# A two-layer graph attention kernel: the last product's blocks written by ScalarE before x is added by accumulating transfers, the first norm taken tile by tile, and another fixed order

## The chip, the cores and the metric

The kernel runs on one core of a Trainium2 chip. The metric is the device time of one execution in microseconds. The kernel before takes 2771.11 us (median of 3 executions, 2768.26 to 2773.03).

## What is computed

There are 32 graphs of 512 nodes with 512 features. Each is normalised, passed through ReLU and two graph attention layers (4 heads of 256, then 1 head of 512), and added to its input. All of it is float32.

```python
def gat_layer(x, mask, W, a_src, a_dst, bias, concat):
    xl = (x @ W).reshape(B, N, H, F)
    asrc = jnp.einsum('bnhf,hf->bnh', xl, a_src)
    adst = jnp.einsum('bnhf,hf->bnh', xl, a_dst)
    e = jax.nn.leaky_relu(asrc[:, :, None, :] + adst[:, None, :, :], 0.2)
    e = jnp.where(mask[..., None], e, NEG_INF)
    attn = jax.nn.softmax(e, axis=1)
    out = jnp.einsum('bsdh,bshf->bdhf', attn, xl)
    ...
h = jnp.maximum(_layernorm(x, axis=-1), 0.0)
mask = (adj > 0) | jnp.eye(N, dtype=bool)[None]
h = jax.nn.elu(gat_layer(h, mask, W1, att_src1, att_dst1, b1, concat=True))
h = gat_layer(h, mask, W2, att_src2, att_dst2, b2, concat=False)
return x + h
```

## The kernel before

**The work of a graph.** Four products are made on TensorE, each as seven smaller ones (a Winograd form of Strassen's scheme): the first projection (`project1`), the first layer's sums over neighbours (`gather1`, four heads), the second projection (`project2`) and the second layer's sums (`gather2`). The sums and differences of blocks that this scheme needs before a product are made by VectorE; its results come out of the 8 PSUM banks (`mm`) by ScalarE or VectorE, and some of them go back into another bank by ScalarE, to be added to.

**The softmax.** `first` finds the softmax's sums row by row: ScalarE forms `l` from a broadcast row `as`, VectorE masks it, ScalarE exponentiates it. The result goes through DRAM to become a row that every partition has (`drr<-rr`, `rr<-drr`). `second` builds the attention block `p` on VectorE from `rr`, adds the mask to it by accumulating transfers from DRAM (`p<-dm`, queue of POOL), and exponentiates it on ScalarE. `p` is what `gather1` and `gather2` multiply with.

**The last product and the residual.** `gather2` makes four output tiles of 128 rows, each from two column halves. `residual` first loads the four tiles of x into the four slots `t` (SP's queue). Each partial product that comes out of a bank is then multiplied by the softmax's share and added into its half of a tile by one VectorE instruction (in `put`, cost `PUT`). After the last of them the tile is stored by SP and its slot is given back. The slots `t` also hold VectorE's differences t1 and t2 for `gather1`, so the next graph's `gather1` waits for the stores.

**The turn.** After the first graphs, a turn of the loop does `gather1` and `second` of one graph, `project1` of the next but one, `gather2` of the current one, the norm of the third next (`norm`, `norm_turn`), and `project2`. The parts of a turn are interleaved.

**What sets the order.** Every function only records jobs with their engine, their cost and the keys they read and write (`Program.add`). `Program.order` then lays the jobs out. In the kernel before it is a planner: it runs through a time of its own, with costs, DMA delays (`KIND`) and the numbers `PLACES` as ranks, and lets each engine take the ready job of the lowest rank. The numbers of one turn serve for all turns. Each engine runs its jobs in the order that comes out, and a job that waits holds up everything behind it on its engine or queue.

**The start.** The norm of graph 0 computes the statistics of its four tiles, one power on POOL for all four (`L770`), then ScalarE's ReLU, TensorE's transposes (`identf`) and the copies into `ht`. The first products need `ht`, four blocks of W1 and the columns that VectorE computes from W1 and the attention vectors (`scores1`, 8 instructions for a first pair of columns).

Of the kernel before, what the change touches and what calls it, by code (L numbers as in the profile page):

```python
# [10 lines left out]
F32 = mybir.dt.float32  # L11
# [4 lines left out]
OP = mybir.AluOpType  # L16
# [28 lines left out]
class Banks(Slots):  # L45
# [171 lines left out]
)  # L217
LATE = {
   
}  # L220

# [1488 lines left out]
```

## Time and profile before

| | us |
|---|---|
| median of 3 executions | 2771.11 |
| lowest, highest | 2768.26, 2773.03 |
| profiled execution, whole time | 2769.33 |
| its span, first to last instruction | 2767.6 |
| VectorE busy | 2558.2 (92%) |
| ScalarE busy | 2229.1 (81%) |
| POOL busy | 313.1 (11%) |
| DMA, share of 16 engines: queue of SP / queue of POOL | 42.4% / 25.1% |

The durations come from the profiled execution, which is 1.8 us under the median of the runs. Each 128x128 by 128x256 float32 matmul shows as two instructions, which overlap in the pipeline: a single one lasts about 380 ns, while a new one starts about every 210 ns. So TensorE's busy time says when it had something in work, not how fast it went; how many matmuls a stretch of fixed length holds says that. Names such as `t<-mm,rs,t` say what an instruction writes and reads. "p<-dm" is the transfer that adds the mask, "as<-das" and "rr<-drr" are the broadcasts.

### The profile page before, as it was taken

Reading aid. Unit: us, or ns where it says so; the run is one execution under the profiler, and the core shown is the slowest. Engines: PE = TensorE matmul, PEld = TensorE weight load, DVE = VectorE, ACT = ScalarE, POOL = GpSimd, SP = SyncE. Lnnn points to the kernel's source line nnn. Section 1 sums busy time; section 2 is a strip of 40 time slices with the busy share of each in tenths; the row PEclk is TensorE's granted clock in tenths of the full one; section 3 lists DMA queues with packets and bytes.
Section 4 is the critical chain, followed back from the end, with each engine's and each line's share of the span. In section 5 each row is a group of like instructions: output and inputs, shape, how many; then the busy total and the mean of one; then the engine's idle time right before and its main releaser. Section 6 shows DMA issues by size and latency. Waiting matters only on the chain. (4 is left out here: it accounts for less than half of the span.)

```text
span 2767.6 us, 42320 instructions
## 1 busy us (share of the span) xinstructions
PE 2742.4 (99%) x12924; PEld 2371.8 (86%) x12924; DVE 2558.2 (92%) x6732; ACT 2229.1 (81%) x4907; POOL 313.1 (11%) x356
## 2 busy tenths in 40 slices
PE   7999999999999999999999999999999999999999
PEld 6788888888888888888888888888888888888887
DVE  8999999999999999999999999999999999999996
ACT  5978888778887788877888877888778788788883
POOL 0110111101111111111011111111111111101110
PEclk9999999999999999999999999999999999999999
DMA  8657766667666667667676766766676767767563
GB/s 232 176 157 182 203 167 184 187 176 194 182 183 179 182 176 196 178 175 195 173 201 172 182 187 178 192 186 180 180 188 175 201 167 180 195 165 208 162 171 112
DMA packets 375864, 502.14 MB, mean 181 GB/s; under 512 B 222804, under 2 KB 227668, under 8 KB 375636
## 3 DMA queue, kind: packets, MB, share of 16 engines
q1 hardware_dynamic: 329844, 332.68, 42.4%
q0 software_dynamic: 45792, 166.74, 25.1%
q8 instruction: 103, 1.69, 0.3%
q14 instruction: 125, 1.02, 0.1%
HBM read 316.41 MB, written 51.31 MB: 133 GB/s over the span
## 5 line engine op out<-in xcount | busy, mean ns | idle before, releaser
L531 PE MATMUL mm<-w_sb,hs 128*128 128x257 f32 (+3 forms) x2908 | 667.0, 367 | 5.1 <-ACT mm L514 3.3
L531 PEld LDWEIGHTS mm<-w_sb,hs 128*128 128x128 f32 x2908 | 539.7, 190 | 87.7 <-ACT mm L514 6.7
L525 POOL DMA_DIRECT2D p<-dm x314 | 273.2, 875 | 2295.0 <-DVE p L517 764.3
L531 PE MATMUL mm<-w_sb,ht 128*128 128x258 f32 x2112 | 528.6, 382 | 2.7 <-ACT mm L514 2.5
L531 PE MATMUL mm<-p,xl 128*128 128x258 f32 (+1 forms) x1984 | 495.8, 383 | 0.1
L531 PE MATMUL mm<-w_sb,h 128*128 128x257 f32 x2056 | 477.8, 379 | 0.0
L517 DVE SCALAR_TENSOR_TENSOR p<-rr,z 128x512 f32<-128x512 f32 (+1 forms) x636 | 456.0, 742 | 2.4 <-DMA rr<-drr 2.4
L531 PEld LDWEIGHTS mm<-w_sb,ht 128*128 128x128 f32 x2112 | 393.7, 190 | 63.6 <-ACT mm L514 6.4
L514 ACT ACTIVATE p<-p,z 128x512 f32<-128x512 f32 (+1 forms) x636 | 433.4, 720 | 17.7 <-DVE p L517 12.4
L531 PEld LDWEIGHTS mm<-w_sb,h 128*128 128x128 f32 x2056 | 389.0, 189 | 58.4 <-ACT xl L514 0.5
L531 PEld LDWEIGHTS mm<-p,xl 128*128 128x128 f32 x1984 | 367.2, 190 | 52.7 <-issue 6.0
L514 ACT ACTIVATE mm<-mm 128x257 f32<-128x257 f32 (+2 forms) x498 | 169.8, 347 | 269.2 <-PE mm L531 236.2
L514 ACT ACTIVATE l<-as,z 128x512 f32<-128x512 f32 x516 | 354.4, 716 | 30.8 <-DMA as<-das 30.7
L514 ACT ACTIVATE l<-l,low 128x512 f32<-128x512 f32 x516 | 370.3, 721 | 7.6 <-DVE low L517 6.7
L517 DVE CUSTOM_DVE_ANT_1 l<-l,mt 128x512 f32<-128x512 f32 x516 | 346.2, 681 | 28.4 <-ACT l L514 27.4
L514 ACT ACTIVATE xl<-mm 128x258 f32<-128x258 f32 (+2 forms) x748 | 269.3, 382 | 91.4 <-PE mm L531 89.8
L514 ACT ACTIVATE h<-mm,b_sb 128x256 f32<-128x256 f32 (+1 forms) x504 | 231.0, 480 | 77.3 <-PE mm L531 76.6
L531 PE MATMUL mm<-t,hs 128*128 128x258 f32 (+1 forms) x992 | 246.1, 380 | 0.0
L517 DVE TENSOR_TENSOR xl<-xl,mm 128x258 f32<-128x258 f32 x372 | 155.3, 419 | 57.9 <-PE mm L531 48.3
L531 PEld LDWEIGHTS mm<-t,hs 128*128 128x128 f32 x992 | 185.8, 190 | 25.5 <-DVE t L517 0.2
L531 PE MATMUL mm<-xl,p 128*128 128x258 f32 (+2 forms) x752 | 189.7, 388 | 1.0 <-ACT h L514 0.6
L517 DVE SCALAR_TENSOR_TENSOR h<-xr,h 128x512 f32<-128x512 f32 x256 | 172.2, 683 | 6.1 <-ACT xr L514 6.1
(137 smaller groups left out, 3706.2 us busy)
## 6 DMA issues: line engine op xcount, KB each, us to landing
p<-dm POOLq DMA_DIRECT2D x314, 512.0 KB, 5.0
rr<-drr SPq DMA_DIRECT2D x159, 512.0 KB
x<-in_x_dram SPq DMA_DIRECT2D x129, 256.0 KB
adj<-in_adj_dram SPq DMA_DIRECT2D x128, 256.0 KB
as<-das SPq DMA_DIRECT2D x64, 512.0 KB
t<-in_x_dram SPq DMA_DIRECT2D x124, 256.0 KB
out_dram<-t SPq DMA_DIRECT2D x124, 256.0 KB
dm<-m SPq DMA_DIRECT2D x64, 256.0 KB
```

Of the source, the lines that this page charges most:

```text
L514: prog.add("ACT", cost, reads, writes, lambda: nc.scalar.activation(*a, **k))
L517: prog.add("DVE", cost, reads, writes, lambda: f(*a, **k))
L525: lambda: nc.gpsimd.dma_start(to, at, accum_op=OP.add), size,
L531: f(*a, **k)
```

## The change

**The residual.** `residual` no longer loads x, except for the last graph, whose last product is made in another way (`gather2_plain`). `put` lets ScalarE write the first partial product of each half of a tile, scaled by the share, and leaves VectorE only the second ones (products 3 and 7). When a tile is complete, a new accumulating transfer on POOL's queue adds x from DRAM to it, and the store follows.

**The first norm.** For graph 0, the epsilon, the power on POOL and the shift are done for each tile by itself; for the others they stay in one piece.

**The identity.** `identf` is no tile of its own any more but lies in a part of `hx`, which is first used otherwise when graph 1 has been transposed. The transposes therefore read the key of `hx`.

**The order.** The planner is gone. The numbers `PLACES` are new, finer by a factor of 100, and are the order itself: each engine takes its jobs in the order of their numbers.

```diff
-    identf = sbuf.tile([P, P], F32, name="identf")
-    make_identity(nc, identf)
...
+    identf = hx[SMALL[0]][:, 0, :]
+    make_identity(nc, identf)
...
-        every = [sk + (t,) for t in range(NT)]
-        rstd = st[:, :, S + A]
-        dve(TINY, every, every, nc.vector.tensor_scalar_add, rstd, st[:, :, S + 1], EPS)
-        prog.add(
-            "POOL", 1.0, every, every,
-            lambda: nc.gpsimd.tensor_tensor(rstd, rstd, half, op=OP.pow),
-        )
...
+        for ts in ([t] for t in range(NT)) if b == 0 else [range(NT)]:
+            every = [sk + (t,) for t in ts]
+            at = slice(ts[0], ts[-1] + 1)
+            rstd = st[:, at, S + A]
+            dve(TINY, every, every, nc.vector.tensor_scalar_add, rstd, st[:, at, S + 1], EPS)
+            prog.add(
+                "POOL", 1.0, every, every,
+                lambda r=rstd, n=len(every): nc.gpsimd.tensor_tensor(r, r, half[:, :n], op=OP.pow),
+            )
...
-            dma(XLOAD, [x2_key(b, 0, 0)], halves, xr, x[b, d * P : (d + 1) * P, :])
+            if b == B - 1:
+                dma(XLOAD, [x2_key(b, 0, 0)], halves, xr, x[b, d * P : (d + 1) * P, :])
+            else:
+                for c in range(2):
+                    prog.alias(xk + (c,), [xk, xk + (c,)])
...
-            dve(
-                PUT, [bk, sk, xk + (c,)], [xk + (c,)], nc.vector.scalar_tensor_tensor,
-                to, ps[:, :M], share, to, op0=OP.mult, op1=OP.add,
-            )
+            if n in (3, 7):
+                dve(
+                    PUT, [bk, sk, xk + (c,)], [xk + (c,)], nc.vector.scalar_tensor_tensor,
+                    to, ps[:, :M], share, to, op0=OP.mult, op1=OP.add,
+                )
+            else:
+                act(COPY, [bk, sk, xk], [xk + (c,)], to, ps[:, :M], AF.Copy, scale=share)
...
+                halves = [xk, xk + (0,), xk + (1,)]
+                accumulate(XADD, halves, halves, xt, x[b, d * P : (d + 1) * P, :])
                 dma(STORE, [xk, xk + (0,), xk + (1,)], (), out[b, d * P : (d + 1) * P, :], xt)
...
     def order(self):
-        jobs, rank = self.jobs, self.ranks()
...
+        jobs, rank, done = self.jobs, list(self.ranks()), []
...
+        for j in sorted(range(len(jobs)), key=lambda j: (rank[j], j)):
+            lines[jobs[j][0]].append(j)
...
+            q = min((q for q in lines if q and not left[q[0]]), key=lambda q: rank[q[0]])
+            j = q.popleft()
```

Over the whole program ScalarE gets 248 instructions more (128x256, out of PSUM), VectorE 248 fewer of them and 6 small ones more in the first norm, POOL 124 transfers of x and 3 powers more, and SP 124 loads of x fewer. TensorE's matmuls are the same in number and shape.

**POOL in a steady turn.** Before, from the mask of the second layer's `p` on, over the masks of the next graph's head 0 and head 1, the power of a norm, to the mask of head 2 (each mask in two transfers):

```order
L525 DMA p_104<-dm_121 128x1024 x2
L525 DMA p_102<-dm_120 128x1024 x2
L525 DMA p_103<-dm_120 128x1024 x2
L770 TENSOR_TENSOR stats_123<-stats_123,half 128x4
L525 DMA p_104<-dm_120 128x1024 x2
```

And now, the same stretch:

```order
L481 DMA p_101<-dm_119 128x1024 x2
L481 DMA p_102<-dm_121 128x1024 x2
L481 DMA t_108<-in_x_dram 128x512
L481 DMA t_106<-in_x_dram 128x512
L481 DMA t_107<-in_x_dram 128x512
L729 TENSOR_TENSOR stats_122<-stats_122,half 128x4
L481 DMA t_105<-in_x_dram 128x512
L481 DMA p_103<-dm_121 128x1024 x2
L481 DMA p_101<-dm_121 128x1024 x2
```

The masks of head 1, which stood ahead of the power, now stand behind it and behind all four additions of x.

**SP in a steady turn.** The four stores of the output, and the transposes (`L811`, now `L770`) that bring a later graph's normalised tiles `x` into `ht`. Before:

```order
L520 DMA rr_114<-drr_118 128x1024
L520 DMA out_dram<-t_108 128x512
L520 DMA x_90<-in_x_dram 128x512
L520 DMA out_dram<-t_106 128x512
L520 DMA out_dram<-t_109 128x512
L520 DMA out_dram<-t_107 128x512
L811 DMA_TRANSPOSE x_91<-adj_94 128x8x128
L520 DMA drr_119<-rr_115 4x8x32
L811 DMA_TRANSPOSE x_90<-adj_95 128x8x128
L520 DMA rr_115<-drr_119 128x1024
```

Now:

```order
L476 DMA x_88<-in_x_dram 128x512
L476 DMA drr_117<-rr_113 4x8x32
L476 DMA out_dram<-t_108 128x512
L476 DMA out_dram<-t_106 128x512
L476 DMA out_dram<-t_105 128x512
L770 DMA_TRANSPOSE x_87<-adj_93 128x8x128
L476 DMA out_dram<-t_107 128x512
L770 DMA_TRANSPOSE x_88<-adj_94 128x8x128
L476 DMA rr_113<-drr_117 128x1024
L770 DMA_TRANSPOSE x_89<-adj_93 128x8x128
```

The stores still stand just ahead of the transposes, but each now also waits for an addition of x on POOL's queue.

**The start, on SP's queue.** Before (`x` are graph 0's tiles, `p` the attention vectors, `w_sb` W1):

```order
L520 DMA w_sb<-in_L_gnn_W_dram 128x2x256
L520 DMA x_90<-in_x_dram 128x512
L520 DMA x_88<-in_x_dram 128x512
L520 DMA x_91<-in_x_dram 128x512
L520 DMA x_89<-in_x_dram 128x512
L520 DMA p_102<-in_L_gnn_att_src_dram 128x512
L520 DMA w_sb<-in_L_gnn_W_dram 128x2x256 x3
L520 DMA p_102<-in_L_gnn_att_dst_dram 128x512
```

Now:

```order
L476 DMA x_88<-in_x_dram 128x512
L476 DMA x_87<-in_x_dram 128x512
L476 DMA b_sb<-in_L_gnn_b_dram 128x8x1
L476 DMA x_89<-in_x_dram 128x512
L476 DMA x_90<-in_x_dram 128x512
L476 DMA w_sb<-in_L_gnn_W_dram 128x2x256
L476 DMA p_101<-in_L_gnn_att_src_dram 128x512
L476 DMA w_sb<-in_L_gnn_W_dram 128x2x256 x2
L476 DMA p_101<-in_L_gnn_att_dst_dram 128x512
L476 DMA w_sb<-in_L_gnn_W_dram 128x2x256 x5
```

The bias b1, a transfer of single 4-byte elements that was the 28th, is now third. The second attention vector is still the tenth transfer, now ahead of the fourth block of W1 instead of behind it.

More of the change, by code (lines that the diff above doesn't have):

```diff
@@ L2 @@
 from contextlib import ExitStack
-from heapq import heappop, heappush
 import concourse.bass as bass
@@ L63 @@
 PLACES = (
[153 rows of a table removed]
-)
-LATE = {
-}
[197 rows of a table added]
+)
 class Program:
-    CROSS, SAME = 0.15, 0.07
-    PAIRS = {("PE", "ACT"): 0.21, ("PE", "DVE"): 0.21, ("DVE", "POOL"): 0.58, ("POOL", "DVE"): 0.4}
-    AHEAD, MASK, OTHER = 3.5, (0.75, 1.84), 0.76
-    KIND = {
-        0.3: (0.39, 1.21, 0.1, 0.9),
-        0.76: (0.81, 1.62, 0.33, 0.64),
-        0.77: (0.44, 1.45, 0.2, 0.82),
-        0.9: (0, 1.72, 1.0, 0.41),
-        0.92: (0.48, 2.18, 0.24, 0.89),
-        0.94: (-0.2, 1.76, 0.21, 0.6),
-        1.09: (1.58, 1.56, 0.53, 0.59),
-        1.84: (0.48, 2.18, 0.24, 0.89),
-        2.23: (0.58, 1.62, 0.53, 0.4),
-    }
     ENGINES = "PE", "ACT", "DVE", "POOL", "SP"
@@ L286, in ranks @@
         turn = sum(job[1] for job in self.jobs[first : first + each] if job[0] == "PE")
-        rank, self.place = [], []
         for j in range(n):
             if j < first:
-                v, i = j, 0
+                yield PLACES[j] / 10000
             elif j < last:
-                v, i = first + (j - first) % each, (j - first) // each + 1
+                yield PLACES[first + (j - first) % each] / 10000 + turn * ((j - first) // each + 1)
             else:
-                v, i = first + each + j - last, (last - first) // each + 1
-            self.place.append(v)
-            rank.append(PLACES[v] / 100 + turn * i)
-        return rank
+                yield PLACES[first + each + j - last] / 10000 + turn * ((last - first) // each + 1)
     def order(self):
-        jobs, rank = self.jobs, self.ranks()
-        n = len(jobs)
-        after = [[] for _ in range(n)]
+        jobs, rank, done = self.jobs, list(self.ranks()), []
+        after, left = [[] for _ in jobs], [len(job[2]) for job in jobs]
         for j, job in enumerate(jobs):
@@ L305, in order @@
                 after[d].append(j)
-        left = [len(job[2]) for job in jobs]
-        ready_at, self.start, done = [0.0] * n, [0.0] * n, []
-        free, soon, ready = dict.fromkeys(self.ENGINES, 0.0), defaultdict(list), defaultdict(list)
-        wires, now, behind = {"SP": deque(), "POOL": deque()}, 0.0, {"SP": 0.0, "POOL": 0.0}
-        for j in range(n):
-            if not left[j]:
-                heappush(soon[jobs[j][0]], (0.0, j))
-        def release(j, at):
-            for s in after[j]:
-                ready_at[s] = max(ready_at[s], at(s))
-                left[s] -= 1
-                if not left[s]:
-                    heappush(soon[jobs[s][0]], (ready_at[s], s))
@@ L321, in step @@
-        def step(until):
-            nonlocal now
-            busy = [q for q in wires if wires[q] and wires[q][0][1] <= now]
-            speed = dict.fromkeys(wires, 1.0)
-            if len(busy) == 2:
-                speed["SP"], speed["POOL"] = self.kind(wires["SP"][0][0])[2:]
-            event, which = until, None
-            for q in wires:
-                if wires[q]:
-                    j, since, todo = wires[q][0]
-                    t = now + todo / speed[q] if q in busy else since
-                    if t < event:
-                        event, which = t, q
-            for q in busy:
-                wires[q][0][2] -= (event - now) * speed[q]
-                behind[q] -= (event - now) * speed[q]
-            now = event
-            if which in busy:
-                j = wires[which].popleft()[0]
-                release(j, lambda s: event + self.kind(j)[1] + LATE.get(self.place[j], 0) / 100)
-            return which is not None
@@ L344, in order @@
-        while len(done) < n:
-            t, e = float("inf"), None
-            for q in self.ENGINES:
-                if ready[q]:
-                    at = free[q]
-                elif soon[q]:
-                    at = max(free[q], soon[q][0][0])
-                else:
-                    continue
-                if q in wires:
-                    at = max(at, now + behind[q] - self.AHEAD)
-                if max(at, now) < t:
-                    t, e = max(at, now), q
-            if step(t):
-                continue
-            while soon[e] and soon[e][0][0] <= t:
-                k = heappop(soon[e])[1]
-                heappush(ready[e], (rank[k], k))
-            j = heappop(ready[e])[1]
-            self.start[j] = t
-            free[e] = t + jobs[j][1]
-            done.append(j)
-            if jobs[j][4] is not None:
-                wires[e].append([j, free[e] + self.kind(j)[0], jobs[j][4]])
-                behind[e] += jobs[j][4]
-            else:
-                release(j, lambda s: t + jobs[j][1] + self.latency(j, s))
+        lines = {e: [] for e in self.ENGINES}
@@ L371, in order @@
+        for j in sorted(range(len(jobs)), key=lambda j: (rank[j], j)):
+            lines[jobs[j][0]].append(j)
+        lines = [deque(q) for q in lines.values()]
+        while any(lines):
+            q = min((q for q in lines if q and not left[q[0]]), key=lambda q: rank[q[0]])
+            j = q.popleft()
+            done.append(j)
+            for k in after[j]:
+                left[k] -= 1
         return done
@@ L443, in tile_gat @@
     nc.scalar.preload_act_table_set("natural_log_exp_and_others")
-    identf = sbuf.tile([P, P], F32, name="identf")
-    make_identity(nc, identf)
-    diag = sbuf.tile([P, P], BF16, name="diag")
-    nc.vector.tensor_scalar(diag, identf, -1.0, BIG, op0=OP.add, op1=OP.mult)
     half = sbuf.tile([P, NT], F32, name="half")
@@ L468, in tile_gat @@
     hx = {n: sbuf.tile([P, 3, P], F32, name=f"hx{n}") for n in SMALL}
+    identf = hx[SMALL[0]][:, 0, :]
+    make_identity(nc, identf)
+    diag = sbuf.tile([P, P], BF16, name="diag")
+    nc.vector.tensor_scalar(diag, identf, -1.0, BIG, op0=OP.add, op1=OP.mult)
     rs = sbuf.tile([P, 2, 2, 2], F32, name="rs")
@@ L557, in tile_gat @@
     ROWS = {4: 1.09, 8: 2.23}
+    XADD = 1.9
     COPY, ADD, TINY = 0.266, 0.335, 0.08
@@ L790, in norm_turn @@
             pe(
-                [xk], [pk], 0.44,
+                [xk, ("hx", SMALL[0])], [pk], 0.44,
                 [(nc.tensor.transpose, (pt[:, k * P : (k + 1) * P], hn[:, k * P : (k + 1) * P], identf), {})
```

18 lines of the change are left out of this document (5 added, 13 removed), and 350 rows, old and new, of the table PLACES.

## The prediction

> **What bounds the kernel now.** I read the page first, for what TensorE leaves idle.
>
> ```profile
> span 2767.6 us, 42320 instructions
> PE 2742.4 (99%) x12924; PEld 2371.8 (86%) x12924; DVE 2558.2 (92%) x6732; ACT 2229.1 (81%) x4907; POOL 313.1 (11%) x356
> ```
>
> TensorE has work in flight in all but 25.2 us, and the change leaves its matmuls as they are. So it can win only what TensorE loses now, and the question is where that is. The table of windows gives the ends and the first turns, the table of waits who is waited for:
>
> ```profile
> core 0: us, PE busy (x) PEld busy (x) DVE busy (x) ACT busy (x) POOL busy (x), PEclk, DMA share, GB/s
> 0.00:12.06 12.06, 0.00 (x0) 0.00 (x1) 5.88 (x22) 2.15 (x3) 1.74 (x7) 1.00 0.79 235
> 12.06:60.00 47.94, 45.45 (x210) 39.02 (x211) 42.55 (x178) 27.73 (x62) 1.12 (x1) 0.96 0.88 254
> 60.00:300.00 240.00, 238.68 (x1070) 196.39 (x1069) 222.41 (x597) 203.84 (x449) 32.66 (x35) 1.00 0.66 173
> 2595.00:2695.00 100.00, 98.79 (x464) 84.77 (x463) 93.67 (x235) 84.14 (x185) 12.18 (x14) 1.00 0.63 164
> ...
> PE mm L531 <- ACT x L514: 12.1, 1, 12.1
> PE mm L531 <- ACT mm L514: 5.8, 10, 1.2
> ```
>
> 12.1 us pass before the first matmul, and most of the other waits end with a copy on ScalarE (`mm`). In the steady turns the busy time hides losses, since matmuls overlap; the number that a window of fixed length holds does not. I cut 300 to 2595 us into 27 windows of 85 us, about a turn each:
>
> ```profile
> 300.00:385.00 85.00, 85.00 (x407) 74.29 (x406) 79.68 (x208) 69.66 (x154) 9.76 (x11) 1.00 0.68 182
> ...
> 725.00:810.00 85.00, 84.56 (x402) 73.44 (x402) 79.09 (x206) 69.07 (x154) 9.76 (x11) 1.00 0.69 182
> 810.00:895.00 85.00, 84.19 (x403) 73.46 (x402) 79.73 (x207) 69.28 (x155) 9.76 (x11) 1.00 0.70 182
> ...
> 980.00:1065.00 85.00, 83.82 (x400) 72.93 (x399) 78.90 (x203) 68.36 (x153) 9.79 (x11) 1.00 0.68 182
> ...
> 2340.00:2425.00 85.00, 84.53 (x401) 73.13 (x400) 79.02 (x204) 68.95 (x154) 9.79 (x11) 1.00 0.70 183
> ...
> sum 2295.00, PE 2290.57 PEld 1998.29 DVE 2146.94 ACT 1886.80 POOL 263.62; mean PE 84.84 PEld 74.01 DVE 79.52 ACT 69.88 POOL 9.76
> ```
>
> A fed window holds 407, that is 0.209 us a matmul. The four short ones shown lack 5, 4, 7 and 6; all 27 together lack 39, or 8.1 us. That is all that the steady turns can give. What a loss looks like, on ScalarE and TensorE in the worst window:
>
> ```profile
> 1000.46 1.33 ACT L514 ACTIVATE p<-p,z 128x512 f32<-128x512 f32 x2 [1.37 <-DMA p<-dm]
> ...
> 1002.01 0.49 PE L531 MATMUL mm<-w_sb,hs 128*128 128x129 f32 x2 [1.18 <-ACT mm L514]
> ```
>
> A mask's transfer lands late, the exponential that needs it holds ScalarE, the copies behind it come late, and TensorE waits 1.18 us. ScalarE's own waits in the steady turns say which causes recur:
>
> ```profile
> ACT l L514 <- DMA as<-das: 28.3, 31, 2.3
> ACT mm L514 <- DVE t L517: 25.6, 27, 1.8
> ACT p L514 <- DMA p<-dm: 5.2, 8, 1.4
> ```
>
> Transfers again, and once a turn VectorE's write of an output block (`t`), which holds a bank that ScalarE wants to fill.
>
> **The change part by part.** First the partial products that leave VectorE. Their durations, with the nearest row for the new ScalarE form (a copy of almost the same size out of PSUM) and POOL's issue:
>
> ```profile
> L517 DVE SCALAR_TENSOR_TENSOR t<-mm,rs,t 128x256 f32<-128x256 f32 x320 | 147.3, 474 | 6.3 <-PE mm L531 5.3
> ...
> L514 ACT ACTIVATE xl<-mm 128x258 f32<-128x258 f32 x496 | 177.0, 383 | 70.5 <-PE mm L531 69.3
> ...
> L525 POOL DMA_DIRECT2D p<-dm x314 | 273.2, 875 | 2295.0 <-DVE p L517 764.3 <-DVE t L517 596.2 <-PE mm L531 450.2
> ```
>
> A turn has 12 of them; 8 move. VectorE loses 8 x 0.474 = 3.8 us a turn and goes from 79.5 to 75.7 of 85. ScalarE gains 8 x 0.383 = 3.1 us and goes from 69.9 to 72.9. Neither sets the end by its sum, so 3.8 us a turn is not the gain. What the move can give is that ScalarE no longer waits for VectorE's `t` once a turn. It can also take: a scaled copy needs the reciprocal that VectorE makes, and ScalarE, on which TensorE waits, has 12 us of air a turn instead of 15. The other half of the gain must come from the new order, which can put more work between a transfer and the instruction that waits for it. Bounds for the steady turns: 8.1 us if every loss goes, nothing if losses as many come back (worse is the third rival). I take two thirds, 5.4, since one of the three recurring waits goes for certain, and the other two are waits in a queue that an order can move.
>
> Then the additions of x. In the stretch around the end of a `gather2`:
>
> ```profile
> q0 software_dynamic: 576, 2.10, 29.9%
> ...
> p<-dm POOLq DMA_DIRECT2D x4, 512.0 KB, 5.3
> ...
> 1130.00:1160.00 30.00, 30.00 (x140) 26.14 (x139) 26.96 (x68) 27.01 (x56) 4.52 (x5) 1.00 0.73 192
> ```
>
> Four masks take 29.9% of the 16 DMA engines for 30 us, 2.24 us each. A tile of x has half a mask's bytes at its target and as many at its source, so 1.12 to 2.24 us, and four of them 4.5 to 9.0 us in a stretch that has 27% of 30 us, 8.1 us, free. The four loads that go away were issued earlier in the turn and free nothing here. The additions run after the last use of the tile, and their cover is the time until the slots `t` and the masks behind them in the queue are needed. How long that is:
>
> ```profile
> 1139.75 0.86 POOL L525 DMA_DIRECT2D p<-dm  x1 [4.17 <-PE mm L531]
> 1142.60 0.86 POOL L525 DMA_DIRECT2D p<-dm  x1 [1.99 <-DVE p L517]
> ...
> 1143.52 0.45 DVE L517 SCALAR_TENSOR_TENSOR t<-mm,rs,t 128x256 f32<-128x256 f32 x1
> ...
> 1152.42 1.34 ACT L514 ACTIVATE p<-p,z 128x512 f32<-128x512 f32 x2
> ...
> 1153.19 0.69 DVE L517 TENSOR_TENSOR t<-p 128x512 f32<-128x512 f32 x1
> ...
> 1156.07 2.76 PE L531 MATMUL mm<-t,hs 128*128 128x258 f32 x12
> ```
>
> The first mask of head 1 is issued at 1139.75 and lands some 5.3 us later, at 1145.1. Two exponentials (1.34) and VectorE's difference (0.69) must follow before TensorE uses it at 1156.07. So 1156.07 - 2.0 - 1145.1 = 9.0 us are cover. The additions take 4.5 to 9.0 of them: I cost them at nothing, with ScalarE's other work as the cover. POOL's issues, 4 x 0.875 = 3.5 us a turn on an engine that is busy for 9.8 of 85, cost nothing by themselves, and the stores behind them on SP are covered in the same way.
>
> The Trainium skill speaks against the move in one point (DMA: Bandwidth & Descriptors, section "SWDGE vs HWDGE vs iDMA"): inside a DMA engine transfers issued by GpSimd and those issued by SP stand in different queues, and the engine takes them in turn. By that, a load of x on SP's queue shared the engine with the masks, while an addition of x stands in front of them; no row here shows this sharing. Another section of that page ("Anatomy of one DMA") gives 2.0 us plus bytes over 436 GB/s for a GpSimd transfer: as an estimate 2.6 us for x and 3.2 us for a mask. The row has 5.3 us for the mask, so the measurement decides and the larger cost stands.
>
> The start. Which transfer is waited for, and what TensorE then loses:
>
> ```profile
> 13.21 0.43 DVE L517 SCALAR_TENSOR_TENSOR xr<-w_sb,p 128x256 f32<-128x256 f32 x1 [1.30 <-DMA p<-in_L_gnn_att_dst_dram]
> ...
> 14.67 1.57 PE L531 MATMUL mm<-w_sb,ht 128*128 128x258 f32 x4
> ...
> 49.40 1.65 PE L531 MATMUL mm<-w_sb,hs 128*128 128x258 f32 x4 [1.32 <-DVE hs L517]
> ```
>
> The first product starts at 14.67, when VectorE has used the second attention vector, not when the norm is done. So the norm by tiles alone wins nearly nothing: before that product stand the same 2.5 MB of loads as now. The bias in third place delays them. A later wait (1.32 us at 49.40) and a granted clock of 0.96 over 47.94 us, 1.9 us, can be won by an order that feeds TensorE better there, 3.2 us in all. The bias cannot cost more than the 1.3 us that VectorE now waits for the vector, taken once more. Bounds: 3.2 better to 1.3 worse; I take 1.0 better. The stretches 60 to 300 and 2595 to 2695 have 1.3 and 1.2 us idle: 0 to 2.5 better, I take 1.0.
>
> The end:
>
> ```profile
> 2756.64 8.33 SPq L520 DMA_DIRECT2D out_dram<-t  x4
> ...
> 2763.92 0.69 DVE L517 TENSOR_TENSOR t<-mm,t 128x512 f32<-128x512 f32 x1 [1.89 <-PE mm L531]
> ```
>
> The last store's issue ends at 2764.97 and the span at 2767.6. Now four additions fall into this stretch, and the stores that wait for them stand ahead of the last tile's on SP. The additions' 4.5 us at the least fit beside 14 us of the last plain product; if the last two are late, the end waits for about one of them, up to 2.2 us. I take 0.5 worse.
>
> Sum: -5.4 - 1.0 - 1.0 + 0.5 = -6.9 us. The profiled execution took 2769.3 us, so 2762.4 us; the median of the runs is 1.8 us above it: 2764 us.
>
> **The rivals.** *Nothing comes of it, 2771 us.* VectorE's air is not what TensorE waited for, and transfers come as late as before; ScalarE's 3.1 us more a turn take back what its shorter wait gives. For it speaks that two of the three recurring waits are for transfers, and that the change adds some; against it that the order is new on all engines. The case that the order does not do what it is said to do ends here too.
>
> *The additions come before the masks, 2800 us.* Head 1's masks now stand behind the four additions and a power, and the additions wait for the last partial product. If that stays where it is (its VectorE write ends at 1143.97), the masks are issued 3.5 + 1.1 us later, at 1148.6 instead of 1139.75. That takes 8.8 of the 9.0 us of cover, and what is left of the additions' 4.5 to 9.0 us after the 4.6 us of issuing, 0 to 4.4 us, comes late on ScalarE, and after it on TensorE, in each of 29 turns: 0 to 128 us. At 1 us a turn it is 2771 + 29 = 2800 us. It decides from the point where the delay of the masks passes 9.0 us. Against it: the order may have the last partial products earlier in the turn.
>
> *Start and end cost more than the turns give, 2776 us.* The bias and the additions at the end at their upper bounds, 1.3 + 2.2 us, and a gain of nothing between, 2771.1 + 3.5 = 2775; one more wait of 1.3 us on VectorE at the start makes it 2776.
>
> **How the numbers follow.** A measurement of this kernel tells about 0.2%, 5.5 us, from no change: faster is below 2765.6, slower above 2776.6. Forecast: 0.58. Its own range is 2757 to 2771, and it lies close to the bound, so 0.46 of it is faster and 0.12 within. Nothing comes of it: 0.15, all within. The additions before the masks: 0.22, all slower. Start and end: 0.05, 0.01 of it within and 0.04 slower. That makes 0.46 faster, 0.28 within, 0.26 slower. The range is 2753 to 2790: below it lies only a gain of nearly every bound at once (8.1 + 3.2 + 2.5 = 13.8 us and more), above it the dearer part of the second rival.
>
> **What would show it.** Right: windows of 85 us with 407 matmuls nearly throughout; the wait of ScalarE's `mm` for VectorE's `t` gone; VectorE near 75.7 and ScalarE near 72.9 us a window; a first product with `w_sb` between 13.5 and 15 us. Wrong: one wait that comes back in each turn, of ScalarE for `p<-dm` or of VectorE for a store of `t`, with 402 matmuls or fewer in most windows; additions of x that take far more than 2.24 us; a store of an output tile that ends well after the last matmul.

## The result and the profile after

The changed kernel takes 2805.57 us (median of 4 executions, 2803.67 to 2812.98); the kernel before, run beside it, 2769.69 us (2764.25 to 2773.03). The ratio is 1.0136, with an interval of 1.0111 to 1.0162: it is 1.4% slower. The prediction said 2764 us, slightly faster, with a range of 2753 to 2790; the time lies outside it.

The page of the kernel after, span and busy times:

```profile
span 2802.4 us, 42502 instructions
...
PE 2756.4 (98%) x12924; PEld 2377.9 (85%) x12924; DVE 2485.0 (89%) x6490; ACT 2329.8 (83%) x5155; POOL 432.9 (15%) x483
```

The matmuls are as many as before and the span is 34.8 us longer. VectorE has less to do and ScalarE more, as the change says. TensorE's busy time is 14 us longer for the same matmuls, which as before hides a part of what it loses. The windows of 85 us show how much that is, and where (busy time of each engine with the number of instructions, granted clock, DMA share, GB/s):

```profile
300.00:385.00 85.00, 84.78 (x405) 74.21 (x404) 77.10 (x200) 73.13 (x163) 13.67 (x15) 1.00 0.71 183
...
980.00:1065.00 85.00, 83.13 (x395) 72.18 (x394) 75.73 (x196) 70.83 (x158) 12.19 (x14) 1.00 0.70 179
...
2170.00:2255.00 85.00, 82.83 (x392) 71.75 (x391) 74.21 (x191) 70.28 (x154) 13.65 (x15) 1.00 0.71 178
...
sum 2295.00, PE 2273.24 PEld 1979.49 DVE 2054.51 ACT 1949.57 POOL 360.53; mean PE 84.19 PEld 73.31 DVE 76.09 ACT 72.21 POOL 13.35
```

The kernel before has 407 and 400 matmuls in the first two of these windows. Its row for the third:

```profile
2170.00:2255.00 85.00, 85.00 (x408) 74.38 (x407) 79.46 (x207) 69.86 (x155) 9.76 (x11) 1.00 0.67 183
```

Windows that held 407, 400 and 408 matmuls hold 405, 395 and 392. All 27 together lack 180 against 39 before; at 0.209 us each that is 37.6 us against 8.1. The granted clock is 1.00 in these rows, so it is not the clock. The loss lies in the steady turns, and in nearly all of them: 28 of the 29 counted below are longer than the same turn before.

The trace says the same by the start of the matmul of the same number in both kernels (not always the same product, since the order differs in places). A turn is 404 matmuls. Against before, matmul 404 starts 0.66 us later, matmul 808 1.76, matmul 12524 32.83, the last 34.11; the span ends 34.8 later. So the 29 turns from matmul 808 to 12524 cost 31.07 us, 1.07 us each (85.14 us before, 86.21 now), the start and first turns 1.8, the last 400 matmuls, from number 12524 on, 1.3 and the tail behind the last matmul 0.8.

What TensorE waits for now that it did not wait for before, from the table of waits (us in total, times, longest):

```profile
PE mm L487 <- ACT xl L470: 12.5, 15, 1.4
...
PE mm L487 <- ACT f L470: 6.7, 29, 0.4
...
PEld mm L487 <- ACT xl L470: 21.0, 21, 1.8
...
PEld mm L487 <- ACT f L470: 13.4, 36, 0.6
```

Two waits for copies on ScalarE, one of them once in every turn (29 times). The same table for VectorE and ScalarE, and behind it the row of the kernel before that answers to the first:

```profile
DVE stats L473 <- DMA x<-in_x_dram: 38.8, 25, 3.0
...
DVE t L473 <- DMA out_dram<-t: 9.4, 19, 1.3
...
ACT x L470 <- DVE stats L473: 40.0, 26, 5.7
...
ACT mm L470 <- DVE t L473: 41.2, 28, 1.7
```

```profile
DVE stats L517 <- DMA x<-in_x_dram: 6.9, 8, 3.2
```

VectorE's statistics wait for a load of x 25 times where they did 8 times, and the ReLU of ScalarE waits for the statistics 26 times. The wait of ScalarE's `mm` for VectorE's `t`, which was to go, is still there.

**The wait for `f`.** One turn on ScalarE and TensorE (start, duration, engine):

```profile
507.73 0.26 ACT L470 ACTIVATE mm<-mm 128x129 f32<-128x129 f32 x1
507.91 1.32 ACT L470 ACTIVATE p<-p,z 128x512 f32<-128x512 f32 x2
508.84 0.39 PE L487 MATMUL mm<-w_sb,hs 128*128 128x129 f32 x2
509.13 0.27 ACT L470 ACTIVATE f<-mm 128x129 f32<-128x129 f32 x1
509.45 0.49 PE L487 MATMUL mm<-wx,hx 128*128 128x129 f32 x2 [0.22 <-ACT f L470]
```

The product `mm<-wx,hx` does not read `f`. It writes one half of a bank (129 columns), and the copy `f<-mm` reads the other half of the same bank. The program's own list of dependences knows the halves as two keys and orders nothing between them, but the built program makes the product wait for the copy. In the new order the copy stands behind two exponentials `p`, 1.32 us, on ScalarE; before, it stood ahead of them, as one turn of the kernel before shows:

```profile
588.25 0.28 ACT L514 ACTIVATE f<-mm 128x129 f32<-128x129 f32 x1
588.42 0.28 ACT L514 ACTIVATE mm<-mm 128x129 f32<-128x129 f32 x1
588.62 1.32 ACT L514 ACTIVATE p<-p,z 128x512 f32<-128x512 f32 x2
```

Counted over 24 turns by the gaps between matmul starts, this costs 0.49 us in each.

**The wait for `xl`.** Another place of the turn, over POOL, SP, VectorE, ScalarE and TensorE:

```profile
801.79 0.86 POOL L481 DMA_DIRECT2D t<-in_x_dram  x1 [1.26 <-ACT l L470]
802.79 0.33 SPq L476 DMA_DIRECT2D x<-in_x_dram  x1
803.48 1.77 POOL L481 DMA_DIRECT2D t<-in_x_dram  x2 [0.83 <-ACT t L470]
...
810.65 0.69 DVE L473 BATCH_NORM_STATS2 stats<-x 128x6 f32<-128x512 f32 x1 [2.58 <-DMA x<-in_x_dram]
...
811.86 1.46 POOL L729 TENSOR_TENSOR stats<-stats,half 128x4 f32<-128x4 f32 x1 [6.60 <-DVE stats L473]
...
813.56 0.81 ACT L470 ACTIVATE x<-x,stats 128x512 f32<-128x512 f32 x1 [2.44 <-DVE stats L473]
...
817.77 0.63 ACT L470 ACTIVATE xl<-mm 128x257 f32<-128x257 f32 x2
...
818.18 1.57 PE L487 MATMUL mm<-w_sb,hs 128*128 128x257 f32 x6 [1.40 <-ACT xl L470]
```

The chain starts with a plain load of x for a later graph's norm, issued on SP at 802.79 when its slot comes free. Three additions of x are issued on POOL around it, at 801.79 and 803.48. The load lands about 7.8 us after its issue, VectorE's statistics wait 2.58 us for it, POOL's power for the statistics, ScalarE's ReLU (`x<-x,stats`) for the power. In the new order two of these ReLUs stand ahead of two copies `xl<-mm`, and TensorE waits 1.40 us for those. In the kernel before the ReLUs stood behind the copies:

```profile
548.39 0.65 ACT L514 ACTIVATE xl<-mm 128x257 f32<-128x257 f32 x2
...
550.34 0.38 ACT L514 ACTIVATE xl<-mm 128x257 f32<-128x257 f32 x1
550.61 1.53 ACT L514 ACTIVATE x<-x,stats 128x512 f32<-128x512 f32 x2
```

In 17 of 24 turns the load is late enough to matter, and it costs 0.65 us a turn. Turn by turn the loss is what the landing exceeds 6.05 us by, cut off at zero: a load that lands after 7.1 us costs 1.01, one after 6.5 us 0.40, one after 6.0 us nothing.

What TensorE loses behind late masks is left as it was, 0.24 us a turn against 0.29, although ScalarE itself waits for masks 9.5 us in all against 5.2. So 0.49 + 0.65 - 0.05 = 1.09 us account for the 1.07.

### The profile page after: what moved, and what is told of

The parts are those of the page before. It is cut to its first block, busy times and chain, and to the rows that moved or that the text cites. A ratio compares the mean times of both kernels' runs of the same rounds, so it can differ in the third digit from the quotient of the medians.

```text
span 2802.4 us, 42502 instructions
## 1 busy us (share of the span) xinstructions
PE 2756.4 (98%) x12924; PEld 2377.9 (85%) x12924; DVE 2485.0 (89%) x6490; ACT 2329.8 (83%) x5155; POOL 432.9 (15%) x483
## 3 DMA queue, kind: packets, MB, share of 16 engines
q14 instruction: 125, 1.02, 0.1%
## 5 line engine op out<-in xcount | busy, mean ns | idle before, releaser
L487 PE MATMUL mm<-w_sb,hs 128*128 128x257 f32 (+3 forms) x2908 | 670.9, 368 | 19.8 <-ACT xl L470 12.5
L481 POOL DMA_DIRECT2D p<-dm x314 | 282.5, 932 | 2042.9 <-DVE p L473 992.4
L487 PE MATMUL mm<-w_sb,ht 128*128 128x258 f32 x2112 | 522.4, 382 | 0.6 <-ACT mm L470 0.5
L487 PE MATMUL mm<-p,xl 128*128 128x258 f32 (+1 forms) x1984 | 507.1, 384 | 0.1
L470 ACT ACTIVATE xl<-mm 128x258 f32<-128x258 f32 (+2 forms) x748 | 262.5, 378 | 65.2 <-PE mm L487 61.5
```

What stands on the lines that cost most here:

```text
L470: prog.add("ACT", cost, reads, writes, lambda: nc.scalar.activation(*a, **k))
L481: lambda: nc.gpsimd.dma_start(to, at, accum_op=OP.add), size,
L487: f(*a, **k)
```

## The experiments

Each kernel was timed in five rounds beside the kernel before, and each ratio is against that. In the diffs `PLACES[1153 + n]` is the number of job n of the repeated turn; a job with a smaller number comes earlier on its engine.

**The copy `f` back ahead of the exponentials.** Job 255 is the copy, 257 the `mm<-mm` in front of the exponentials.

```diff
+PLACES = [*PLACES]
+PLACES[1153 + 255] = PLACES[1153 + 257] - 1
```

> One ScalarE copy per steady turn (f<-mm) is moved ahead of two exponentials, to just before the copy mm<-mm of the same bank. Theory: TensorE's product with wx cannot write into the bank until that copy has read the other half of it, and the copy stands 1.3 us too late in ScalarE's order; this costs 0.39 + 0.10 = 0.49 us in each of 29 turns. Then about 14 us go: 2791 us, and the wait of PE mm for ACT f disappears from the steady turns. Rival: that product waits for the copy mm<-mm, which does not move, and the profile names the wrong releaser; then the time stays at 2805 within 3 us.

2786.51 us, ratio 1.0069 (1.0055 to 1.0083), 19 us less than after. The waits of this kernel:

```profile
PE mm L487 <- ACT f L470: 0.4, 1, 0.4
...
DVE stats L473 <- DMA x<-in_x_dram: 36.4, 26, 2.3
```

The wait for `f` falls from 29 times to one. The late load stays. The gain is larger than the expected 14 us: a turn is 0.68 us shorter, of which the wait for `f` is 0.49. Most of the rest was lost behind late masks; why that shrank as well is not shown.

**The two ReLUs of the norm, and the copy `adj<-x` behind them, back behind the copies `xl`.**

```diff
+PLACES[1153 + 458] = PLACES[1153 + 435] + 1
+PLACES[1153 + 454] = PLACES[1153 + 435] + 2
+PLACES[1153 + 455] = PLACES[1153 + 435] + 3
```

> Three ScalarE jobs of the norm (two ReLUs x<-x,stats, one adj<-x) are moved behind the two copies xl<-mm that TensorE waits for; the additions of x stay. Theory: the last of the norm's four loads of x lands 5.2 to 8.3 us after its issue, and what exceeds 6.0 us holds the ReLUs and with them the copies; 0.65 us a turn, 29 turns, so 19 us go: 2787 us, though VectorE still waits for x as often. Rival (the additions hurt through the masks behind them on POOL's queue, or through the stores): the time stays at 2805 within 4 us.

2792.49 us, ratio 1.0085 (1.0071 to 1.0099). The late load no longer reaches TensorE ("PE mm <- ACT xl", 12.5 us in the kernel after, is gone from the table), though VectorE waits for it nearly as long as before; but a turn won 0.45 us, less than the 0.65:

```profile
DVE stats L473 <- DMA x<-in_x_dram: 35.7, 27, 3.2
...
DVE t L473 <- DMA out_dram<-t: 22.6, 22, 2.3
```

VectorE now waits 22.6 us for stores of `t` to leave their slots, where the kernel after has 9.4: the additions and the stores behind them are late for the next use of the slots. The wait ends when one addition is moved forward, as the kernel with that move shows below; that the other wait had covered this is argued, not shown.

**Both**, the edits of the first and the second kernel together.

> The two moves together. Theory: the losses are independent, 14 + 19 us go, 2772 us, so the time of the kernel before within 5 us. Rival (ScalarE's 3.1 us more a turn are what is lost, and a stall that is removed comes back at the next tight place): no better than 2790.

2780.65 us, ratio 1.0041 (1.0028 to 1.0054): more than the expected 2772. The two gains, 0.68 and 0.45 us a turn, make 0.80 together, so they are not independent. The same wait for the stores is what is left (25.2 us), and TensorE loses 0.145 us a turn behind it.

```profile
DVE t L473 <- DMA out_dram<-t: 25.2, 21, 2.6
```

**After without the additions.** The order stays as it is in the changed kernel, POOL issues no addition, so the output of all graphs but the last lacks x.

```diff
-                accumulate(XADD, halves, halves, xt, x[b, d * P : (d + 1) * P, :])
+                prog.add("POOL", 0.0, halves, halves, lambda: None, XADD)
```

> The four transfers that add x to the output tiles of a turn are left out, so the output lacks x; the order of everything else stays. Theory of the late load: without 3 additions at its side the last load of x lands in 5.2 to 6.0 us in every turn, and 0.65 us a turn go, 19 us: 2787 us; the wait for f stays. Rival (the order alone is at fault, since the load is issued when its slot comes free and the norm then has no time left): at most 4 us go, 2802 us. A second rival (the additions also delay masks and stores): more than 22 us go, under 2783.

2786.47 us, ratio 1.0067 (1.0054 to 1.0079), as expected.

```profile
DVE stats L473 <- DMA x<-in_x_dram: 2.7, 2, 1.8
...
PEld mm L487 <- ACT f L470: 13.3, 35, 0.6
```

The load is now ready when its slot in VectorE's order comes, 5.2 us after its issue, in 26 of 27 turns; the wait for `f` is untouched. So the additions make the load late, and the wait for `f` has nothing to do with them.

**Both moves and one addition earlier.** The addition of the last tile (job 393) goes ahead of the norm's power on POOL, which waits for the late load; in the changed kernel it stands behind it.

```diff
+PLACES[1153 + 393] = PLACES[1153 + 416] - 1
```

> The two moves, and the addition of the tile that stood behind the norm's power on POOL (#393) moved ahead of it. Theory: with the two moves the next wait is VectorE's t for the store of an output tile (25.2 us in all, 21 times), and TensorE loses 0.15 us a turn behind it; that addition is ready 9 us before the power and waits only for its place in the queue. Then VectorE's wait falls below 10 us and 3 to 5 us go: ratio to the kernel before about 1.0025 instead of 1.0041. Rival (what is late is the additions' own 7 us of landing, not their place): VectorE's wait stays over 18 us, the time within 2 us.

2771.61 us, ratio 1.0011 (1.0002 to 1.0021): better than expected. Windows of this kernel:

```profile
980.00:1065.00 85.00, 85.00 (x407) 74.59 (x406) 76.92 (x200) 73.18 (x163) 13.63 (x15) 1.00 0.72 183
...
sum 2295.00, PE 2292.60 PEld 2008.89 DVE 2083.42 ACT 1979.70 POOL 367.81; mean PE 84.91 PEld 74.40 DVE 77.16 ACT 73.32 POOL 13.62
```

407 matmuls where the changed kernel has 395; the 27 windows lack 32, fewer than the 39 of the kernel before. VectorE's wait for stores of `t`, 25.2 us in the kernel with two moves, is gone from the table. The late load itself is as late as ever, and no longer matters:

```profile
DVE stats L473 <- DMA x<-in_x_dram: 42.1, 28, 2.3
```

With five numbers of the order changed, almost all of the loss is gone. What is left against before, by matmul starts: the 29 turns are 2.7 us shorter, the start and the first turns 1.3 us longer, the last 400 matmuls 2.8 us longer, the tail 0.8 us. This compares one trace with one trace, while the executions of the kernel before range from 2764.25 to 2773.03 us; so the 2.7 us are not shown to be a gain.

**The first two moves without the additions** (the edits of the third and the fourth kernel; output without x, as there), to see what the additions cost where they stand well.

> The two moves, and the additions of x left out (the output lacks x). Theory: what is left above the kernel before comes from the additions, through the stores and VectorE's t; 8 to 12 us go, ratio 0.9995 to 1.0015, and VectorE waits for no store. Rival (the rest is the order's own): ratio 1.003 or more.

2774.62 us, ratio 1.0015 (1.0006 to 1.0023), no better than the kernel with the additions and all three moves. One of its turns loses 7.2 us to a mask that landed 9.1 us after its issue; without that turn a turn is 84.96 us long, against 84.93 in the kernel with all three moves, counted over the same 24 turns. In the right place the additions cost the steady turns nothing. At the end they do: from matmul 12524 to the last it takes 95.1 us before and 95.3 here, but 96.4 in the changed kernel and 97.9 with the three moves.

**The first two moves with the residual of before.** x is loaded by SP as soon as a slot is free, VectorE does all partial products and no addition is made. The diff shows three places; `prog.load`, left out here, issues a load on SP as soon as the jobs that used its slot before are issued.

```diff
+                prog.load(
+                    halves, lambda xr=xr, d=d: nc.sync.dma_start(xr, x[b, d * P : (d + 1) * P, :])
+                )
...
-                act(COPY, [bk, sk, xk], [xk + (c,)], to, ps[:, :M], AF.Copy, scale=share)
+                prog.add(
+                    "ACT", COPY, [bk, sk, xk], [xk + (c,)],
+                    lambda: nc.vector.scalar_tensor_tensor(
+                        to, ps[:, :M], share, to, op0=OP.mult, op1=OP.add
+                    ),
+                )
...
-                accumulate(XADD, halves, halves, xt, x[b, d * P : (d + 1) * P, :])
+                prog.add("POOL", 0.0, halves, halves, lambda: None, XADD)
```

> The two moves, with the residual as in the kernel before: x loaded by SP into the slots t as soon as they are free, all partial products added by VectorE, no addition on POOL; the new order otherwise. Theory: the new residual is what costs, the order with its two places mended is as good as the old one or a little better; ratio 0.998 to 1.001. Rival (the order is the worse one by itself): 1.003 or more.

2983.72 us, ratio 1.0776 (1.0761 to 1.0791). This is no fair comparison, and the waits say why: the loads wait on SP for their slots, and the broadcasts `rr` and `as` stand behind them.

```profile
DVE p L485 <- DMA rr<-drr: 106.9, 31, 5.6
...
ACT l L482 <- DMA as<-das: 128.0, 31, 8.3
```

**All three moves, the first partial products on VectorE.** Only the engine of those eight instructions a turn changes; additions and order stay.

```diff
-                act(COPY, [bk, sk, xk], [xk + (c,)], to, ps[:, :M], AF.Copy, scale=share)
+                prog.add(
+                    "ACT", COPY, [bk, sk, xk], [xk + (c,)],
+                    lambda: nc.vector.tensor_scalar_mul(to, ps[:, :M], share),
+                )
```

> The three moves (ratio to the kernel before 1.0011), with the first partial products multiplied by the share on VectorE instead of ScalarE, at the places where ScalarE had them in the order of emission; the additions stay. Theory: which engine writes them sets nothing; within 4 us of the three moves, ratio 0.9995 to 1.0026, although ScalarE loses 3.1 us of work a turn and VectorE gets 3.8 us. Rival (ScalarE's air of 12 us a turn instead of 15 makes TensorE wait): at least 6 us faster, under 0.999. Second rival (VectorE's relief was a gain that the transfers hid): at least 6 us slower, over 1.0033.

2827.96 us, ratio 1.0215 (1.02 to 1.0231). The theory that the engine makes no difference fell. A turn is 1.73 us longer than with the three moves alone:

```profile
PE mm L487 <- DVE t L473: 16.9, 30, 1.8
...
ACT mm L470 <- DVE t L473: 115.1, 29, 4.0
```

In this order VectorE has no room for the eight instructions at that place, and ScalarE waits for its `t` once a turn, up to 4.0 us. The same change on top of the first two moves alone has no measured time.

**All three moves, the old residual with its loads behind the broadcasts on SP.** As above, with each load held back until a broadcast of its turn is issued.

```diff
+                behind = [prog.marks[-1] + (89, 165, 183, 183)[d]] if b < B - 3 else []
+                prog.load(
+                    halves, behind,
+                    lambda xr=xr, d=d: nc.sync.dma_start(xr, x[b, d * P : (d + 1) * P, :]),
+                )
```

> The three moves, with the residual of the kernel before: x loaded by SP, all partial products added by VectorE, no addition on POOL; the loads now stand behind the broadcasts rr and as on SP's queue instead of ahead of them. Theory: the 203 us of the run before it with this residual came from SP waiting for a slot t ahead of those broadcasts (VectorE's p waited 107 us for rr); they go, and the old residual in this order is within 6 us of the three moves, ratio 0.999 to 1.0033. Rival (this order needs VectorE's relief, whatever the loads do): over 1.01.

2855.31 us, ratio 1.0309 (1.0294 to 1.0325). VectorE's wait for the broadcast `rr` is down from 106.9 us to 5.6, and what remains is the wait for VectorE of the kernel ahead, here 19.8 us on TensorE and 114.9 on ScalarE:

```profile
ACT mm L482 <- DVE t L485: 114.9, 29, 4.0
...
PE mm L499 <- DVE t L485: 19.8, 30, 1.8
```

So it is the eight instructions on VectorE that this order has no room for, with additions or without.

**A fourth move.** Another copy `mm<-mm` (job 125) put ahead of the exponentials, to win a little more on ScalarE.

```diff
+PLACES[1153 + 125] = PLACES[1153 + 60] - 1
```

> The three moves, and the copy mm<-mm of the small products (#125) moved ahead of two exponentials of p that wait for a mask. Theory: the largest wait left in the steady turns is that copy behind a late mask, 0.17 us a turn; most of it goes, 3 to 5 us, ratio 0.9993 to 1.0000. Rival (the exponentials, now later, hold the next product instead): no change or worse, 1.0011 or more.

2800.47 us, ratio 1.0108 (1.0091 to 1.0125): a miss, and a telling one.

```profile
PE mm L487 <- ACT f L470: 27.3, 29, 1.4
```

One turn of it on ScalarE and TensorE:

```profile
924.77 0.26 ACT L470 ACTIVATE mm<-mm 128x129 f32<-128x129 f32 x1 [1.44 <-PE mm L487]
924.95 1.32 ACT L470 ACTIVATE p<-p,z 128x512 f32<-128x512 f32 x2
...
926.44 0.28 ACT L470 ACTIVATE f<-mm 128x129 f32<-128x129 f32 x1
...
926.77 0.49 PE L487 MATMUL mm<-wx,hx 128*128 128x129 f32 x2 [0.95 <-ACT f L470]
```

The moved copy waits 1.44 us on ScalarE for its product, and the two exponentials, which filled that time before, now run behind it. So the copy `f` of this place, behind them in either order, comes later, and the product into the other half of its bank waits, 1.23 us a turn. That a product waits for the copy out of the other half of its bank holds at a second place of the turn.

**Masks earlier** in the turn and in the first turns (jobs 54 and 55 on VectorE, 366 on ScalarE), on top of the three moves.

```diff
+PLACES[1153 + 54] = PLACES[1153 + 53] + 2
+PLACES[1153 + 55] = PLACES[1153 + 53] + 1
+PLACES[366] = PLACES[350] - 1
```

> The three moves (ratio 1.0011), and two more: VectorE makes the last two blocks of p for the mask of head 2 (#54, #55) right behind the first two, ahead of four small jobs, so that the second mask is issued about 1.2 us earlier; and in the first turns one copy mm<-mm (#366) goes ahead of three jobs of the softmax. Theory: the wait that is left in the steady turns (0.17 us a turn, the copy behind exponentials that wait for this mask) mostly goes, 3 to 5 us, and 1.5 us at 63 us; ratio 0.9985 to 0.9995, level with or just under the kernel before. Rival (the four small jobs, 1.3 us later, hold a product of gather1): 1.002 or more.

2772.23 us, ratio 1.0011 (1.0002 to 1.002): no better than the three moves. No kernel run here beats the kernel before.

The starts of matmul 808 and 12524 in each trace, against those of the kernel before, and what that makes of one of the 29 turns between them:

| kernel | 808 (us) | 12524 (us) | a turn (us) |
|---|---|---|---|
| after | +1.76 | +32.83 | +1.07 |
| `f` ahead | +1.37 | +12.77 | +0.39 |
| ReLUs behind | +1.93 | +19.92 | +0.62 |
| both | +0.71 | +8.61 | +0.27 |
| after, no addition | +0.25 | +16.99 | +0.58 |
| both, one addition earlier | +1.28 | -1.46 | -0.09 |
| both, no addition | +3.22 | +6.72 | +0.12 |
| three moves, products on VectorE | +4.10 | +51.60 | +1.64 |
| four moves | +1.42 | +29.20 | +0.96 |
| masks earlier | +2.62 | +2.54 | 0.00 |

## Why the prediction was wrong

**The steady turns: the step that failed first.** "I take two thirds, 5.4, since one of the three recurring waits goes for certain, and the other two are waits in a queue that an order can move." The turns lost 31.07 us in place of winning 5.4. I took a new order as something that could only win back losses that I had listed. It brought two of its own, and 0.49 us a turn of them needs no transfer at all: a copy behind two exponentials, with a product behind the copy because both use one bank. Which instructions stand ahead of that copy could be read from the order before the run; I looked only at the engines' sums and at the waits that the old trace had.

**The additions: the second failed step.** "I cost them at nothing, with ScalarE's other work as the cover." The cover was enough for the masks of head 1, which I had named: TensorE lost no more behind late masks than before. It was the wrong victim. The transfer that became late is a load on another queue, SP's, that is issued in the same microseconds, and its chain runs over VectorE and POOL to two ReLUs which the new order had put in front of copies that TensorE waits for. Without the additions this cost is gone; without the ReLUs in front of the copies it is gone for TensorE as well. Both are needed, as the second and fourth experiments show together. By the rule of the Trainium skill that the prediction cited (DMA: Bandwidth & Descriptors, section "SWDGE vs HWDGE vs iDMA": GpSimd's and SP's transfers stand in different queues of an engine, which takes them in turn) a load on SP shares the engines with the additions. The traces agree: it is in use 5.2 us after its issue without additions beside it, and lands after 5.2 to 8.2 us with them. How the engines divide their time between the two they don't show.

**What ScalarE waits for.** That its wait for VectorE's `t` goes "for certain" was wrong too: it stands at 41.2 us in 28 times over the whole span, against 29.3 in 29 before. The second partial products stay on VectorE, and a bank is still held by them. TensorE did not pay for it: with the three moves its turns are no longer than before, with ScalarE at 73.32 of 85 us.

**The engines' sums came out, VectorE's by luck.** VectorE is at 76.09 us a window (75.7 predicted) and ScalarE at 72.21 (72.9), but with fewer matmuls in the window. With the three moves, where a window holds about as many as before, they are 77.16 and 73.32. VectorE's relief was put too high: its busy time falls by 2558.2 - 2485.0 = 73.2 us for 248 instructions, 0.30 us each and not 0.474. The records of instructions in a row overlap, as the starts and lengths on ScalarE above show (507.73 + 0.26 ends after 507.91), so one that goes frees less than its length. The price of a scaled product on ScalarE was taken from a plain copy, 383 ns; it is 469, of which 2329.8 - 2229.1 = 100.7 us for 248, 0.41 us each, are added to the busy time:

```profile
L470 ACT ACTIVATE t<-mm,rs 128x256 f32<-128x256 f32 x240 | 106.2, 469 | 24.2 <-DVE rs L473 15.7 <-PE mm L487 4.8 <-DMA x<-in_x_dram 0.2
```

**The additions' own size was right.** Queue of POOL:

```profile
q0 software_dynamic: 63648, 199.26, 32.6%
...
t<-in_x_dram POOLq DMA_DIRECT2D x120, 256.0 KB, 7.2
```

Before, the queue took 25.1% of 2767.6 us. (0.326 x 2802.4 - 0.251 x 2767.6) / 124 transfers more is 1.77 us of all engines each, inside 1.12 to 2.24. But an addition lands 7.2 us after its issue, and the bound had said nothing of that.

**The start** gave nothing, where I took 1.0 us. The first product with `w_sb` starts at 14.09 us, inside the predicted 13.5 to 15; but over ten traces with the new start it lies between 13.9 and 15.35, and matmul 404 between 113.6 and 116.6 us, with 114.4 before. "An order that feeds TensorE better there" wasn't found. The other 1.0 us, for the stretches on either side of the steady turns, did not come either: from matmul 404 to 808 the changed kernel takes 1.1 us longer than the kernel before.

**The end** is mis-sized: +0.5 in the sum, and with 2.2 as the bound. It is 1.3 + 0.8 = 2.1 us in the changed kernel, and 2.8 + 0.8 = 3.6 with the three moves; without the additions nearly nothing is lost before the last matmul, while the tail's 0.8 is there without them too.

**The rivals.** The second, 2800 us from 1 us a turn, had the sign and the size (1.07 us a turn), for a reason that did not come about: what TensorE loses behind masks is 0.24 us a turn, no more than before. I gave it 0.22 and argued it away with "the order may have the last partial products earlier in the turn", without looking at what else lies in the same stretch of the queues. Of the signs that were to show the prediction wrong, 402 matmuls or fewer stood in 17 of the 27 windows; but of the waits named beside it, that of ScalarE for masks came 9 times and that of VectorE for stores 19 times, not once in each turn. The gain that the prediction hoped for is small if it is there at all: once the order is mended, the 29 turns of one trace are 2.7 us shorter, those of the last kernel's trace no shorter, and the end takes 3.6. The range's lower end was too low as well: with every bound of the prediction at its best the time is 2771.1 - 13.8 = 2757.3 us, not 2753. Giving the eight instructions back to VectorE in that order costs 1.73 us a turn, so this order uses the relief of VectorE.

**What stays open.** Whether the old residual with an order made for it would beat both: the two runs with it used an order that was made for the new one. Why an addition of 256 KB lands later than a mask of 512 KB.

## What to carry to other kernels

A new order is a change to every engine, and its price is not found by listing the old waits: for each instruction that TensorE waits for, look at what now stands directly ahead of it on its engine, and how late that can be. In the built program two halves of a PSUM bank counted as one thing, so put a copy out of one half ahead of long work when a product into the other half is near. When transfers are added, look for the one that becomes late among all that are issued in the same microseconds, on other queues too, and follow it to the first instruction that has no slack.

## What was unexpected in the hardware

**A bank is waited for as a whole in the built program.** A product into columns of a bank waits for ScalarE's copy out of other columns of the same bank: 0.49 us a turn in the changed kernel, gone when the copy moves ahead, 1.23 us a turn at another place in the kernel with four moves. The Trainium skill (PSUM — Partial Sum Buffer, section "PSUM bank collisions raise a hardware error ⚠️") says that the compiler's back end adds a dependence between instructions of different engines that touch the same bank and quadrant, whatever the address. The traces agree that the wait goes by the bank; what put it there they don't show. The prediction had not drawn on it.

**Accumulating x is slow to land here.** 7.2 us in the median for 256 KB, 4.9 us for a mask of 512 KB on the same queue, though x takes the engines less time (1.77 us against some 2.2).

**One transfer of POOL's queue is late.** The 114th lands after 7.6 us in the kernel before and after 9.0 to 9.2 in the four kernels without additions; where additions are in the queue it took 5.3. In the run with two moves and no additions it alone cost 7.2 us. I have no explanation.
